# Cross-attention on one core: the order of all steps written anew

## The chip, the cores and the metric
The kernel runs on one core of a Trainium2 chip. The core has five engines, which each work through their own instructions in order and wait for each other by semaphores: TensorE (PE in the profile; its weight loads are PEld), VectorE (DVE), ScalarE (ACT), GpSimd (POOL) and SyncE (SP), which here only issues DMAs. The metric is the device time of one execution in microseconds; the median of several runs counts. Times of single instructions come from one further execution, taken with the hardware profiler.

## The reference
```python
B, C1, C2, N = (8, 512, 512, 1024)
D = C2 // 8
q = jnp.einsum('bcn,dc->bnd', x1, Wq) + bq
k = jnp.einsum('bcn,dc->bdn', x2, Wk) + bk[:, None]
v = jnp.einsum('bcn,dc->bdn', x2, Wv) + bv[:, None]
attn = jax.nn.softmax(jnp.einsum('bnd,bdm->bnm', q, k), axis=2)
attn_out = jnp.einsum('bcm,bnm->bcn', v, attn)
return attn_out + x1
```
All in float32. There are eight batches with 1024 query positions n, 1024 context positions m, 512 channels c and 64 dimensions d.

## The kernel before
Each float32 product that matters is made of three passes in a faster format: a tensor is cut into a high part (h), a low part (l) and a combined difference (d), and TensorE multiplies the matching parts into one PSUM bank, with a rescaling of the bank by ScalarE between the passes h, l and the pass d. So each step of the mathematics has a ScalarE and a VectorE step or two around its matmuls.

The work is written as small methods of a class `Batch`, each of which issues one or a few instructions on one engine. A batch has two halves of 512 queries, four quarters Q of 256 queries and eight blocks u of 128 queries; the context is cut into eight tiles i, j or m of 128. The methods, with their lines:

- `ldx1`, `ldx2` (L157 to L170) load the inputs on SP's queue. `Q`, `K` (L205) project; `qe`, `ke` take the results out, `qd`, `kc` copy them to the other partitions by DMA, `qr`, `ql`, `kr`, `kl` split them.
- `S.h.i` (L262, PE) makes the scores of a half and a tile, `Sc.h.i` (L267, ACT) takes them out into the tile `e`.
- `F.Q` (L275 to L278, DVE) folds the scores of a quarter over its tiles, `T.Q` (L282, POOL) takes the maximum over the partitions (`top`), `L.u` (L290, DVE) subtracts it, `E.u` (L293, ACT) takes the exponential in place.
- `H.u` (L297, ACT), `l.u` (L301, DVE) and `d.u` (L306, DVE) split the exponentials of a block into `eh`, `el`, `ed`.
- The softmax's denominator: `es.Q` (L312, ACT) copies half of a quarter's exponentials, `a1.Q` (L315, a DMA issued by POOL) adds the other half to it, `a2.Q` and `a3.Q` (L319, DVE) fold the rest, `tot.Q` (L329, POOL) sums over the partitions into `den`, `few.Q` (L334, two DMAs on SP's queue) turns a row of it into columns, and `rec.Q` (L338, DVE) takes the reciprocal `r`.
- `xh`, `xl`, `xd` (L352 to L362) split the context, `VX.j`, `vf.j`, `VY.j` (L379, L390) make a tile of v in a bank `ps_v`, `vh`, `vl`, `vd` (L401 to L409) take it out in three parts. `VF` (L372) does two tiles of the first batch in full float32.
- `R.u.m` (L418, PE) adds the passes h and l of block u and tile m to the bank `ps_o`, `fx.u` (L430, ACT) rescales it, `D.u.m` (L418) adds the pass d. `lo.u` (L437, SP) loads the bias into an output tile `o`, `oa.u` (L440, a DMA issued by POOL) adds x1 to it, `ev.u` (L447, DVE) adds the bank times the reciprocal, and `st.u` (L457, SP) stores it. For the very last block of all, `ev.7` does the left half and `ew.7` the right half, with a store each (`st.7`, `sw.7`).

The banks `ps_v` and `ps_o` are five in all (`"B": 5`), used in turn. The first matmul of a new block (`R.u.0`) therefore waits until the `ev` of an older block has read its bank, and that `ev` needs its quarter's reciprocal: `a3`, `tot`, `few`, `rec`, `ev`, `R`, over four engines and a DMA.

Nothing decides the order at run time. Three strings, `FIRST` (batch 0), `MIDDLE` (batches 1 to 6, the same words each time) and `LAST` (batch 7), list the steps as words; a + stands for the next batch, a - for the one before. The function `follow` calls them one after the other, and the place in the string is the place in each engine's queue:
```python
    def follow(words, b):
        for word in words.split():
            at = b + {"-": -1, "+": 1}.get(word[0], 0)
            name, *args = word.lstrip("+-").split(".")
            getattr(states[at], name + "_" * (name in fields))(*map(int, args))
```
The steps that read one tensor from PSUM and at most one from SBUF on VectorE are `vl` (L405) and, beside its output tile, `ev` (L447); `rec` reads one small SBUF tensor; all others of VectorE (L275 to L278, L290, L301, L306, L319, L357, L362, L409) read SBUF alone, and two tensors of it.

Of the kernel before, what the change touches and what calls it, by code (L numbers as in the profile page):

```python
# [27 lines left out]


FIRST = """  # L30
wh.0 VF.1.0 wl.0 ldx2.0 wd.0 ldx2.1 wh.1 VF.0.0 VF.1.1 VF.0.1 VF.0.2 wl.1 VF.1.2 xh.1 w4.0 w4.1 xh.2 VF.0.3 xl.1
lwq vf.0 vh.0 VF.1.3 VX.2 xh.3 VX.3 xl.3 vf.1 vh.1 K ldx1.0 xl.2 wd.1 vl.1 vf.2 ldx1.1 Q vf.3 ke kc vl.0 lo.0
xd.1 vd.0 qe xd.2 VX.4 VY.2 qd kr VX.5 kl VY.3 +ldx1.1 vh.2 xd.3 vl.2 vf.4 qr VY.4 vf.5 vh.4 VY.5 vh.3 ql vh.5
S.0.3 Sc.0.3 vl.3 S.0.2 Sc.0.2 S.0.1 S.0.5 vl.4 Sc.0.5 vl.5 S.0.0 Sc.0.1 vd.2 S.0.7 S.0.4 S.1.7 S.1.5 Sc.0.0
S.0.6 Sc.0.4 Sc.0.7 Sc.0.6 F.0 S.1.4 T.0 S.1.0 Sc.1.4 +ldx1.0 S.1.3 vd.1 S.1.1 Sc.1.1 L.0 Sc.1.7 Sc.1.0 +Q L.1
+ldx2.0 S.1.2 E.0 oa.0 +ldx2.1 Sc.1.5 VX.7 E.1 H.0 F.1 vf.7 Sc.1.3 l.0 S.1.6 H.1 VX.6 Sc.1.6 VY.7 R.0.0 R.0.1
es.0 R.0.2 d.0 l.1 T.1 R.0.3 R.0.4 L.3 R.0.5 L.2 vf.6 Sc.1.2 R.1.0 vh.7 VY.6 R.1.1 R.1.2 +qe lo.1 E.3 H.3 d.1
R.1.3 +K E.2 a1.0 es.1 F.2 vl.7 R.1.4 R.1.5 +qd l.3 vh.6 vl.6 H.2 R.3.0 R.3.1 R.3.2 R.3.3 T.2 lo.2 oa.2 lo.3
a1.1 a2.0 R.1.6 R.1.7 R.0.6 R.0.7 fx.1 L.4 E.4 a3.0 H.4 fx.0 oa.1 +qr l.2 F.3 D.1.0 L.5 tot.0 R.2.0 R.2.1 R.3.4
R.2.2 l.4 R.2.3 R.2.4 R.2.5 R.2.6 E.5 few.0 R.2.7 T.3 a2.1 fx.2 d.3 D.0.0 R.3.5 R.3.6 D.0.1 D.0.2 D.0.3 D.0.4  # L40
+ql R.3.7 fx.3 R.4.0 R.4.1 D.1.1 R.4.2 vd.3 L.6 d.2 D.1.2 D.0.5 D.1.3 +ke es.2 D.1.4 D.1.5 D.0.6 a3.1 D.0.7 E.6
rec.0 R.4.3 R.4.4 R.4.5 H.5 R.4.6 H.6 D.2.0 tot.1 D.2.1 D.2.2 R.4.7 fx.4 d.4 D.3.0 D.3.1 D.3.2 D.3.3 D.3.4 +xh.0
ev.0 D.2.3 D.2.4 D.2.5 l.6 D.3.5 R.6.0 a1.2 R.6.1 D.4.0 D.4.1 D.4.2 D.3.6 D.2.6 D.3.7 D.1.6 D.1.7 +kc R.6.2
R.6.3 +kr L.7 E.7 oa.3 l.5 few.1 +kl ev.1 H.7 d.5 R.6.4 R.6.5 st.0 +S.0.7 l.7 +S.0.4 es.3 lo.4 R.5.0 R.6.6 a1.3
D.2.7 +S.0.6 R.5.1 R.5.2 R.6.7 +Sc.0.4 rec.1 ev.3 +Sc.0.7 +S.0.2 R.5.3 +Sc.0.2 +S.0.1 R.5.4 a2.2 a3.2 tot.2
+Sc.0.6 +xh.1 st.1 D.4.3 +S.0.3 +xl.0 ev.2 +xd.0 a2.3 +xl.1 fx.6 +S.0.5 d.6 a3.3 +Sc.0.3 R.7.0 +Sc.0.1 R.7.1
R.5.5 R.5.6 R.5.7 st.3 +VX.1 few.2 +S.0.0 +Sc.0.0 D.4.4 D.4.5 D.4.6 D.4.7 d.7 +S.1.6 D.6.0 oa.4 st.2 fx.5 rec.2
+Sc.0.5 +F.0 D.5.0 tot.3 lo.6 few.3 lo.5 D.5.1 oa.6 D.5.2 +xh.2 R.7.2 D.5.3 D.5.4 R.7.3 R.7.4 D.5.5 R.7.5 lo.7
R.7.6 D.5.6 D.6.1 D.6.2 +T.0 +S.1.0 D.6.3 +Sc.1.6 ev.4 R.7.7 fx.7 +VX.0 +L.0 +S.1.5 +L.1 D.7.0 D.7.1 rec.3 D.6.4
+vf.0 D.5.7 D.6.5 D.6.6 +F.1 oa.5 oa.7 +xl.2 D.6.7 ev.6 +xh.3 +xl.3 ev.5 +vf.1 +E.0 D.7.2 +E.1 st.4 D.7.3 D.7.4  # L50
D.7.5 D.7.6 D.7.7 +VY.0
"""
MIDDLE = """
VY.1 Sc.1.0 es.0 S.1.4 T.1 +ldx1.0 VX.3 -ev.7 xd.1 H.0 -st.7 l.0 vh.1 S.1.1 vl.1 vh.0 H.1 Sc.1.5 VX.5 vf.3 VX.2
xd.3 VY.3 vh.3 VX.4 Sc.1.4 L.3 S.1.3 Sc.1.1 vf.5 vf.2 +ldx1.1 xd.2 Sc.1.3 S.1.7 S.1.2 vl.0 VY.5 a1.0 +Q Sc.1.2
l.1 E.3 vf.4 L.2 -st.6 VY.2 E.2 lo.1 VY.4 Sc.1.7 vh.5 vd.0 vl.3 -st.5 F.2 VX.6 vh.2 H.3 lo.0 vl.5 VX.7 vh.4 l.3
R.1.0 vl.4 vl.2 +ldx2.1 lo.3 T.2 vf.6 +qe R.3.0 +ldx2.0 R.3.1 R.0.0 R.3.2 vf.7 VY.6 a2.0 R.3.3 H.2 L.5 l.2 VY.7
vd.2 R.1.1 oa.1 R.0.1 R.3.4 L.4 vh.6 R.1.2 vd.1 +K E.4 H.4 a3.0 vl.6 R.0.2 d.3 R.0.3 es.1 oa.3 d.0 tot.0 R.1.3
vh.7 vl.7 vd.3 +qd F.3 R.3.5 R.3.6 R.1.4 R.1.5 +qr R.3.7 R.1.6 R.1.7 oa.0 R.0.4 R.0.5 E.5 es.2 R.0.6 d.1 R.0.7
R.2.0 R.2.1 R.2.2 fx.3 l.4 D.3.0 fx.1 H.5 R.2.3 R.2.4 few.0 +ql D.1.0 R.4.0 a1.2 +ke a2.2 a1.1 a3.2 R.4.1 a2.1  # L60
D.1.1 D.1.2 D.1.3 D.1.4 D.1.5 D.1.6 D.1.7 T.3 L.7 a3.1 fx.0 D.0.0 D.0.1 E.7 L.6 E.6 H.6 D.0.2 D.0.3 R.4.2 R.4.3
l.5 D.0.4 +kc D.0.5 D.3.1 D.3.2 D.3.3 R.2.5 R.2.6 tot.1 rec.0 R.4.4 ev.1 R.4.5 R.4.6 R.5.0 D.3.4 D.3.5 D.3.6
D.3.7 R.2.7 +kr es.3 a1.3 st.1 D.0.6 few.1 R.5.1 d.2 l.6 D.0.7 +kl H.7 R.5.2 +S.0.0 R.5.3 fx.2 +S.0.4 +xh.0 lo.2
d.4 l.7 ev.0 +Sc.0.4 rec.1 D.2.0 oa.2 R.4.7 +Sc.0.0 R.5.4 fx.4 ev.3 lo.4 +S.0.2 tot.2 D.2.1 D.2.2 D.2.3 +S.0.3
+S.0.5 +Sc.0.2 +S.0.7 st.0 +Sc.0.3 +Sc.0.7 +S.0.1 oa.4 a2.3 +Sc.0.1 D.4.0 R.5.5 R.5.6 R.5.7 R.6.0 d.6 +Sc.0.5
+S.1.6 +S.0.6 few.2 D.4.1 fx.5 D.4.2 D.4.3 R.6.1 +xl.0 +Sc.0.6 +F.0 D.2.4 st.3 D.2.5 +T.0 R.6.2 d.5 D.2.6 D.2.7
+VX.1 +xd.0 R.6.3 R.6.4 R.6.5 D.4.4 D.4.5 R.6.6 R.6.7 a3.3 lo.5 ev.2 +L.0 D.4.6 D.4.7 +vf.1 st.2 +xh.1 lo.6
R.7.0 +L.1 +Sc.1.6 +S.1.0 tot.3 rec.2 ev.4 d.7 oa.5 +F.1 R.7.1 R.7.2 R.7.3 R.7.4 R.7.5 fx.6 +xh.2 +xl.2 lo.7
D.5.0 +xh.3 R.7.6 +S.1.5 oa.6 D.5.1 oa.7 R.7.7 fx.7 +VX.0 +vf.0 D.6.0 D.6.1 D.6.2 D.6.3 D.6.4 D.6.5 D.5.2 D.5.3
D.6.6 D.6.7 st.4 D.5.4 +xl.3 D.5.5 +xl.1 D.5.6 few.3 D.5.7 D.7.0 D.7.1 rec.3 ev.6 ev.5 D.7.2 +VY.0 D.7.3 +E.1  # L70
D.7.4 D.7.5 +E.0 D.7.6 D.7.7
"""
LAST = """
xd.1 -st.5 T.1 L.3 es.0 H.0 H.1 L.2 -ev.7 xd.2 VX.5 S.1.2 a1.0 Sc.1.5 VY.1 Sc.1.0 Sc.1.2 S.1.7 xd.3 S.1.1 vh.0
E.3 vf.5 S.1.4 -st.6 vh.1 VX.2 l.1 Sc.1.7 Sc.1.1 vf.2 VY.5 lo.0 vl.1 -st.7 S.1.3 vl.0 E.2 Sc.1.4 es.1 l.0 VX.3
lo.3 Sc.1.3 VX.6 VY.2 vf.3 a2.0 H.2 vh.5 vd.0 VX.4 vf.6 F.2 vl.5 T.2 VY.3 vh.2 vh.3 a1.1 vl.2 VY.6 vf.4 VX.7
VY.4 R.0.0 R.0.1 F.3 H.3 R.0.2 vl.3 l.3 vh.6 vf.7 vl.6 a3.0 l.2 vh.4 vl.4 VY.7 R.3.0 R.3.1 R.1.0 R.1.1 R.3.2
R.3.3 R.3.4 L.5 vh.7 vl.7 tot.0 L.4 E.5 R.1.2 R.1.3 R.0.3 d.1 lo.1 a2.1 lo.2 R.3.5 R.2.0 T.3 E.4 es.2 R.0.4
R.0.5 R.0.6 R.0.7 oa.3 L.7 E.7 oa.1 d.2 a3.1 H.5 d.0 R.1.4 vd.1 R.1.5 l.5 L.6 R.1.6 R.2.1 R.3.6 R.1.7 H.4 fx.0
R.2.2 R.2.3 R.2.4 R.2.5 R.2.6 oa.0 few.0 R.2.7 fx.2 R.3.7 d.3 R.5.0 vd.2 R.5.1 vd.3 oa.2 R.5.2 fx.1 tot.1 D.1.0  # L80
few.1 fx.3 D.0.0 l.4 D.0.1 D.0.2 D.0.3 D.2.0 D.1.1 D.3.0 D.3.1 D.3.2 D.2.1 rec.1 D.3.3 E.6 es.3 D.0.4 D.3.4 H.6
l.6 R.5.3 D.0.5 D.0.6 D.0.7 D.3.5 rec.0 D.2.2 D.3.6 H.7 ev.0 D.3.7 a1.2 D.2.3 D.1.2 D.1.3 D.2.4 D.2.5 R.6.0
D.2.6 ev.3 D.1.4 st.0 a1.3 a2.2 a3.2 R.6.1 D.1.5 st.3 D.1.6 R.5.4 D.1.7 ev.1 st.1 R.5.5 R.5.6 D.2.7 lo.5 tot.2
R.6.2 ev.2 few.2 R.4.0 R.6.3 R.6.4 R.4.1 R.4.2 oa.5 a2.3 d.6 R.5.7 fx.5 lo.6 a3.3 R.4.3 d.5 R.4.4 R.6.5 R.6.6
R.6.7 l.7 st.2 R.4.5 R.4.6 lo.7 lo.4 d.4 oa.6 tot.3 few.3 R.4.7 fx.4 rec.2 D.5.0 D.5.1 D.5.2 D.5.3 D.5.4 d.7
R.7.0 D.5.5 R.7.1 R.7.2 R.7.3 R.7.4 rec.3 R.7.5 R.7.6 fx.6 D.4.0 D.5.6 D.6.0 R.7.7 oa.7 D.4.1 D.4.2 D.5.7 ev.5
fx.7 oa.4 st.5 D.4.3 D.4.4 D.4.5 D.4.6 D.6.1 D.7.0 D.7.1 D.7.2 D.4.7 ev.4 st.4 D.7.3 D.7.4 D.7.5 D.7.6 D.7.7
D.6.2 D.6.3 ew.7 sw.7 ev.7 st.7 D.6.4 D.6.5 D.6.6 D.6.7 ev.6 st.6
"""


# [432 lines left out]
```

## Time and profile before

| | us |
|---|---|
| runs: median (lowest to highest of 3) | 667.14 (665.84 to 667.75) |
| the profiled execution's time | 663.9 |
| its span, first to last instruction | 662.1 |
| TensorE busy | 651.1 |
| VectorE busy | 573.0 |
| ScalarE busy | 401.7 |
| GpSimd busy | 207.2 |

The profile names a group of instructions by its line, engine, operation and tiles (out<-in). Busy times overlap between engines; the time is set by whatever the last instruction waited for, step by step. An engine's idle time costs nothing unless another engine waits for it. A span on POOL is rough. The granted clock is TensorE's share of full speed. Times in the timeline count from the span's start.

### The profile page before, as it was taken

How to read it: one execution, taken by the hardware profiler on the slowest of the kernel's cores; microseconds unless marked ns; L12 is line 12 of the kernel's file. 1: busy time of each engine (PE TensorE's matmuls, PEld its weight loads, DVE VectorE, ACT ScalarE, POOL GpSimd, SP SyncE). 2: the span in 40 equal slices, each digit the busy share in tenths (PEclk: the TensorE clock that was granted, in tenths of full speed). 3: DMA queues.
4: the chain of work that ended last, by engine and by line, in shares of the span. 5: the costliest groups of instructions: out<-in, count | busy, mean ns of one | idle time of the engine just before them, and what ended most of it. 6: DMA issues, size and time to landing. Idle time of an engine off the chain costs nothing. (4 is left out here: it accounts for less than half of the span.)

```text
span 662.1 us, 8012 instructions
## 1 busy us (share of the span) xinstructions
PE 651.1 (98%) x2817; PEld 496.6 (75%) x2817; DVE 573.0 (87%) x661; ACT 401.7 (61%) x565; POOL 207.2 (31%) x164
## 2 busy tenths in 40 slices
...
GB/s 320 188 167 136 84 164 253 228 98 127 149 235 190 96 159 165 185 193 104 149 189 176 192 101 160 205 187 165 113 139 234 183 154 113 141 186 38 73 154 155
DMA packets 50551, 106.73 MB, mean 161 GB/s; under 512 B 14160, under 2 KB 14928, under 8 KB 46800
## 3 DMA queue, kind: packets, MB, share of 16 engines
...
q14 instruction: 17, 0.14, 0.1%
...
## 5 line engine op out<-in xcount | busy, mean ns | idle before, releaser
L418 PE MATMUL ps_o<-vh,eh 128*128 128x512 f32 x512 | 200.9, 392 | 5.6 <-DVE o L447 5.6
L418 PE MATMUL ps_o<-vl,el 128*128 128x512 f32 x512 | 200.0, 391 | 0.0
L418 PE MATMUL ps_o<-vd,ed 128*128 128x512 f32 x512 | 141.0, 393 | 0.2 <-DVE vd L409 0.2
L418 PEld LDWEIGHTS ps_o<-vh,eh 128*128 128x128 f32 x512 | 96.3, 188 | 31.8 <-issue 11.7
L418 PEld LDWEIGHTS ps_o<-vd,ed 128*128 128x128 f32 x512 | 96.5, 189 | 21.8 <-DVE vd L409 0.6
L418 PEld LDWEIGHTS ps_o<-vl,el 128*128 128x128 f32 x512 | 96.4, 188 | 20.4 <-DVE el L301 0.2
L282 POOL PARTITION_ALL_REDUCE top<-max x32 | 50.9, 1589 | 190.8 <-DVE max L278 190.8
L329 POOL PARTITION_ALL_REDUCE den<-es x32 | 77.4, 2420 | 95.9 <-DVE es L319 81.8
L301 DVE TENSOR_TENSOR el<-e,eh 128x1024 fp32r<-128x1024 f32 x64 | 86.7, 1355 | 15.2 <-ACT eh L297 15.1
L440 POOL DMA_DIRECT2D o<-in_x1T_dram x64 | 58.3, 949 | 98.1 <-DMA o<-in_bv_dram 83.7
L267 ACT COPY e<-ps_s 128x512 f32<-128x512 f32 x128 | 71.6, 591 | 28.1 <-PE ps_s L262 27.2
L306 DVE SCALAR_TENSOR_TENSOR ed<-eh,el 128x1024 fp32r<-128x1024 f32 x64 | 83.1, 1306 | 1.1 <-PE ps_o L418 1.1
L430 ACT ACTIVATE ps_o<-ps_o 128x512 f32<-128x512 f32 x64 | 37.1, 585 | 74.3 <-PE ps_o L418 74.1
L290 DVE TENSOR_TENSOR e<-e,top 128x1024 f32<-128x1024 f32 x64 | 80.6, 1272 | 1.5 <-POOL top L282 1.5
L293 ACT ACTIVATE e<-e 128x1024 f32<-128x1024 f32 x64 | 66.9, 1056 | 24.2 <-DVE e L290 24.1
L401 ACT ACTIVATE vh<-ps_v 128x512 fp32r<-128x512 f32 x64 | 37.4, 598 | 58.7 <-PE ps_v L379 58.6
L297 ACT ACTIVATE eh<-e 128x1024 fp32r<-128x1024 f32 x64 | 67.4, 1058 | 1.3 <-DVE ed L306 0.7
L379 PE MATMUL ps_v<-wh,xh 128*128 128x512 f32 x248 | 66.9, 391 | 0.0
L379 PE MATMUL ps_v<-wl,xl 128*128 128x512 f32 x248 | 66.3, 389 | 0.0
L379 PE MATMUL ps_v<-wd,xd 128*128 128x512 f32 x248 | 65.4, 392 | 0.0
L447 DVE SCALAR_TENSOR_TENSOR o<-ps_o,r,o 128x512 f32<-128x512 f32 (+1 forms) x65 | 47.5, 740 | 17.5 <-PE ps_o L418 13.2
L390 ACT ACTIVATE ps_v<-ps_v 128x512 f32<-128x512 f32 x64 | 37.2, 593 | 35.6 <-PE ps_v L379 35.4
...
## 6 DMA issues: line engine op xcount, KB each, us to landing
...
```

Source lines behind the costliest of these rows:

```text
L267: nc.scalar.copy(self.half[h][:, :, i, :], self.ps[h, i].rearrange("p (q n) -> p q n", q=2))
L282: nc.gpsimd.partition_all_reduce(self.top[Q], self.fold[Q][:, 0, :], P, ReduceOp.max)
L290: nc.vector.tensor_tensor(e, e, top, ALU.subtract)
L293: nc.scalar.activation(self.unit(u), self.unit(u), AF.Exp)
L297: nc.scalar.activation(self.e[u]["h"], self.unit(u), AF.Copy, scale=SPLIT)
L301: nc.vector.tensor_tensor(self.e[u]["l"], self.unit(u), f32(self.e[u]["h"]), ALU.subtract)
L306: nc.vector.scalar_tensor_tensor(e["d"], f32(e["h"]), -1.0 / T, f32(e["l"]), ALU.mult, ALU.add)
L329: nc.gpsimd.partition_all_reduce(self.den[Q], self.es[Q][:, 0, :], P, ReduceOp.add)
L379: nc.tensor.matmul(self.B[j], self.c[j // 2][z][:, c, ts(j % 2, P)], w[z][:, c, :], start=(start and c == 0), stop=(stop and c == CT - 1), ...
L418: nc.tensor.matmul(self.B[u], self.e[u][z][:, m, :], self.v[m // 2, z][:, m % 2, :], start=start, stop=stop, skip_group_check=True,)
L440: nc.gpsimd.dma_start(self.o[u], x1T[self.b, ts(u, P), :], accum_op=ALU.add)
L447: nc.vector.scalar_tensor_tensor(o, self.B[u][:, at], self.share(u), o, ALU.mult, ALU.add)
```

## The change
All three strings are laid out anew. The set of steps, the methods and the buffers are the same; each engine gets the same instructions in another order. The aim of the new order by its description: the sums and maxima over the partitions (`tot`, `T` on GpSimd) soon meet a step of VectorE that reads PSUM, or a gap. A line of each string:
```diff
 FIRST = """
-wh.0 VF.1.0 wl.0 ldx2.0 wd.0 ldx2.1 wh.1 VF.0.0 VF.1.1 VF.0.1 VF.0.2 wl.1 VF.1.2 xh.1 w4.0 w4.1 xh.2 VF.0.3 xl.1
+VF.0.0 VF.0.1 VF.1.0 VF.1.1 ldx2.0 lwq VF.0.2 ldx2.1 wh.0 wl.0 VF.1.2 wd.0 VF.1.3 wh.1 ldx1.0 w4.0 wl.1 xh.1
...
 LAST = """
-R.2.2 R.2.3 R.2.4 R.2.5 R.2.6 oa.0 few.0 R.2.7 fx.2 R.3.7 d.3 R.5.0 vd.2 R.5.1 vd.3 oa.2 R.5.2 fx.1 tot.1 D.1.0
+fx.1 H.6 l.5 R.5.0 R.5.1 D.1.0 oa.3 tot.1 d.3 D.1.1 D.3.0 fx.0 D.1.2 D.3.1 D.3.2 vd.2 L.7 E.7 vd.3 D.1.3 es.3
```
What the engines get is seen at three places. Names there carry the batch, then the block, quarter or pair of tiles, then a running number: `den_7_1` is the denominator of quarter 1 in batch 7, `r_7_1` its reciprocal, `el_7_5` the low part of block 5.

VectorE in the last batch, from the addition that releases the sum of quarter 1 (the second L319) to the reciprocal that needs this sum. Before:
```order
L319 TENSOR_TENSOR es_7_1_4970<-es_7_1_4970 128x256
L306 SCALAR_TENSOR_TENSOR ed_7_0_5148<-eh_7_0_4896,el_7_0_4972 128x1024
L409 TENSOR_TENSOR vd_7_1_5152<-vh_7_1_5030,vl_7_1_5034 128x1024
L301 TENSOR_TENSOR el_7_5_5156<-e_7_1_4789,eh_7_5_5146 128x1024
L290 TENSOR_TENSOR e_7_1_4789<-e_7_1_4789,top_7_3_5126 128x8x128
L306 SCALAR_TENSOR_TENSOR ed_7_3_5189<-eh_7_3_5064,el_7_3_5069 128x1024
L409 TENSOR_TENSOR vd_7_2_5194<-vh_7_2_5003,vl_7_2_5022 128x1024
L409 TENSOR_TENSOR vd_7_3_5198<-vh_7_3_5071,vl_7_3_5074 128x1024
L301 TENSOR_TENSOR el_7_4_5212<-e_7_1_4789,eh_7_4_5167 128x1024
L338 RECIPROCAL r_7_1_5223<-few_7_1_5207 128x2
```
Now:
```order
L319 TENSOR_TENSOR es_7_1_5019<-es_7_1_5019 128x256
L409 TENSOR_TENSOR vd_7_1_5163<-vh_7_1_5001,vl_7_1_5026 128x1024
L338 RECIPROCAL r_7_0_5175<-few_7_0_5160 128x2
L301 TENSOR_TENSOR el_7_5_5185<-e_7_1_4787,eh_7_5_5153 128x1024
L306 SCALAR_TENSOR_TENSOR ed_7_3_5196<-eh_7_3_5073,el_7_3_5075 128x1024
L409 TENSOR_TENSOR vd_7_2_5204<-vh_7_2_5024,vl_7_2_5040 128x1024
L290 TENSOR_TENSOR e_7_1_4787<-e_7_1_4787,top_7_3_5091 128x8x128
L409 TENSOR_TENSOR vd_7_3_5208<-vh_7_3_5013,vl_7_3_5021 128x1024
L301 TENSOR_TENSOR el_7_6_5217<-e_7_1_4787,eh_7_6_5183 128x1024
L338 RECIPROCAL r_7_1_5228<-few_7_1_5225 128x2
L319 TENSOR_TENSOR es_7_2_5132<-es_7_2_5132 128x512
L319 TENSOR_TENSOR es_7_2_5132<-es_7_2_5132 128x256
```
The reciprocal of quarter 0 has moved from behind that of quarter 1 to the second place after the addition, and the additions of quarter 2 have moved ahead of the first `ev` of the batch.

GpSimd around the same sum. Before:
```order
L440 DMA o_7_3_4983<-in_x1T_dram 128x512
L440 DMA o_7_1_5116<-in_x1T_dram 128x512
L440 DMA o_7_0_4959<-in_x1T_dram 128x512
L440 DMA o_7_2_5119<-in_x1T_dram 128x512
L329 ISA den_7_1_5204<-es_7_1_4970 128x256
L315 DMA es_7_2_5129<-e_7_1_4789 128x1024
```
Now:
```order
L440 DMA o_7_1_4913<-in_x1T_dram 128x512
L440 DMA o_7_3_4958<-in_x1T_dram 128x512
L329 ISA den_7_1_5194<-es_7_1_5019 128x256
L315 DMA es_7_2_5132<-e_7_1_4787 128x1024
L440 DMA o_7_0_4915<-in_x1T_dram 128x512
L440 DMA o_7_2_5171<-in_x1T_dram 128x512
```
Two of the four output DMAs have moved behind the sum; the accumulating DMA of quarter 2 still follows it.

VectorE after the same addition in a middle batch (batch 2). Before:
```order
L319 TENSOR_TENSOR es_2_1_1815<-es_2_1_1815 128x256
L290 TENSOR_TENSOR e_2_1_1464<-e_2_1_1464,top_2_3_1908 128x8x128
L301 TENSOR_TENSOR el_2_5_1926<-e_2_1_1464,eh_2_5_1877 128x1024
L338 RECIPROCAL r_2_0_1941<-few_2_0_1883 128x2
L447 SCALAR_TENSOR_TENSOR o_2_1_1687<-ps_o_2_1_1734,r_2_0_1941,o_2_1_1687 128x512
```
Now:
```order
L319 TENSOR_TENSOR es_2_1_1774<-es_2_1_1774 128x256
L301 TENSOR_TENSOR el_2_5_1934<-e_2_1_1462,eh_2_5_1897 128x1024
L255 TENSOR_TENSOR kl_3_1940<-k_3_1862,kh_3_1938 128x1024
L306 SCALAR_TENSOR_TENSOR ed_2_4_1946<-eh_2_4_1830,el_2_4_1832 128x1024
L338 RECIPROCAL r_2_0_1953<-few_2_0_1873 128x2
L447 SCALAR_TENSOR_TENSOR o_2_0_1807<-ps_o_2_0_1748,r_2_0_1953,o_2_0_1807 128x512
```
The subtraction of the maximum (L290) has moved away, and the splits of the next batch's k (L255) and of block 4 (L306) have moved in ahead of the reciprocal. At the very end, the left and right halves of block 7 (`ev.7`, `ew.7`) are now VectorE's last steps, and `ev.6`, which was last, stands ahead of the `ev` of blocks 5, 4 and 7.

More of the change, by code (lines that the diff above doesn't have):

```diff
@@ L30 @@
 FIRST = """
-wh.0 VF.1.0 wl.0 ldx2.0 wd.0 ldx2.1 wh.1 VF.0.0 VF.1.1 VF.0.1 VF.0.2 wl.1 VF.1.2 xh.1 w4.0 w4.1 xh.2 VF.0.3 xl.1
[L32 to L50, printed above, removed]
@@ new lines @@
+D.3.4 D.3.5 R.4.1 R.4.2 +ke a2.1 d.2 R.4.3 R.4.4 R.4.5 tot.0 vd.3 few.0 R.4.6 L.5 fx.1 D.0.3 D.0.4 D.2.0 D.0.5
+D.0.6 H.6 D.2.1 D.2.2 D.0.7 +kc l.6 +xh.0 rec.0 E.5 R.4.7 a3.1 D.1.0 D.1.1 D.1.2 D.1.3 D.1.4 D.1.5 D.1.6 D.2.3
+es.2 oa.2 H.5 ev.0 L.7 fx.4 E.7 d.4 st.0 D.1.7 R.6.0 D.2.4 D.3.6 tot.1 ev.1 R.6.1 R.6.2 R.6.3 R.6.4 R.6.5 R.6.6
++kr l.5 a1.2 +xl.0 R.5.0 D.2.5 D.4.0 R.5.1 D.3.7 R.6.7 D.2.6 few.1 H.7 +xh.1 R.5.2 R.5.3 D.4.1 d.6 es.3 oa.3
+R.5.4 +kl +S.0.7 d.5 fx.6 +Sc.0.7 +S.0.5 R.5.5 D.2.7 st.1 D.6.0 +S.0.6 +Sc.0.5 a2.2 +xh.3 a3.2 +Sc.0.6 +S.0.3
```

80 lines of the change are left out of this document (47 added, 33 removed).

## The prediction
> **What bounds the kernel now.** I read the engines' shares first, then stretches of the span, then TensorE's waits, and last the order in time around the one large wait. The first line of the page:
> ```profile
> PE 651.1 (98%) x2817; PEld 496.6 (75%) x2817; DVE 573.0 (87%) x661; ACT 401.7 (61%) x565; POOL 207.2 (31%) x164
> ```
> TensorE (PE) is busy for 651.1 of 662.1 us, so all that a new order can win lies in the other 11.0 us and in matmuls that run at a low clock. The table of stretches says where they are (its columns: length, then busy us and count for PE, PEld, DVE, ACT and POOL, granted clock, DMA share, GB/s):
> ```profile
> 0.00:20.00 20.00, 19.02 (x59) 8.96 (x61) 9.23 (x11) 11.73 (x16) 0.19 (x4) 1.00 0.78 275
> 200.00:300.00 100.00, 100.00 (x439) 75.21 (x436) 88.23 (x101) 63.09 (x88) 30.34 (x26) 1.00 0.65 166
> 629.20:634.80 5.60, 0.00 (x0) 0.03 (x1) 2.29 (x5) 0.47 (x1) 0.04 (x1) 0.95 0.79 148
> 634.80:638.10 3.30, 3.30 (x9) 2.63 (x10) 1.54 (x3) 0.00 (x0) 1.63 (x1) 0.57 0.45 160
> ```
> In a middle stretch PE is busy for 100.00 of 100.00 us at full clock. In the last batch it stands still for 5.60 us, and after that it runs for 3.30 us at a clock of 0.57. The list of PE's waits agrees (us in total, times, longest):
> ```profile
> PE ps_o L418 <- DVE o L447: 5.6, 1, 5.6
> PE ps_warm L473 <- DVE spark L468: 1.0, 1, 1.0
> PE ps_o L418 <- DVE vd L409: 0.2, 1, 0.2
> ```
> So there is one wait worth having: a matmul of line 418 waits for VectorE's `ev` (line 447) to free a PSUM bank. From 612 to 635 us the timelines of GpSimd (POOL), VectorE (DVE) and SyncE's queue (SPq) read thus (start, length, what, and in brackets the idle time before it):
> ```profile
> 616.11 10.58 POOL L329 PARTITION_ALL_REDUCE den<-es  x1 [1.83 <-issue]
> ```
> ```profile
> 615.53 0.41 DVE L319 TENSOR_TENSOR es<-es 128x256 f32<-128x256 f32 x1
> 615.87 1.21 DVE L306 SCALAR_TENSOR_TENSOR ed<-eh,el 128x1024 fp32r<-128x1024 f32 x1
> 617.00 1.21 DVE L409 TENSOR_TENSOR vd<-vh,vl 128x1024 fp32r<-128x1024 f32 x1
> 618.13 1.21 DVE L301 TENSOR_TENSOR el<-e,eh 128x1024 fp32r<-128x1024 f32 x1
> ...
> 623.81 1.21 DVE L301 TENSOR_TENSOR el<-e,eh 128x1024 fp32r<-128x1024 f32 x1
> 632.40 0.17 DVE L338 RECIPROCAL r<-few 128x2 f32<-128x2 f32 x1 [7.38 <-DMA few<-den]
> 632.50 1.23 DVE L301 TENSOR_TENSOR el<-e,eh 128x1024 fp32r<-128x1024 f32 x1
> 633.65 0.16 DVE L338 RECIPROCAL r<-few 128x2 f32<-128x2 f32 x1
> 633.91 1.41 DVE L447 SCALAR_TENSOR_TENSOR o<-ps_o,r,o 128x512 f32<-128x512 f32 x2
> ```
> ```profile
> 626.71 1.12 SPq L334 DMA_DIRECT2D few<-den  x2
> ```
> The sum over the partitions of quarter 1 (`tot.1`, line 329) takes 10.58 us. Beside it VectorE issues eight steps without a gap (from 615.87 to 623.81 are seven steps of 1.13 us, the distance of 617.00 and 618.13), and each reads two SBUF tensors. The last of them begins at 623.81 and ends at 625.02; the sum ends at 626.69, 1.67 us later. Then the chain runs to PE: `few` is issued at 626.71, the reciprocal starts at 632.40, `ev` at 633.91, PE at 634.80. How long the same step takes elsewhere (min/median/max in ns):
> ```profile
> L329 POOL PARTITION_ALL_REDUCE den<-es x32: 1786/2064/10580, 58.4 to 646.4; - x32
> L282 POOL PARTITION_ALL_REDUCE top<-max x32: 1056/1746/1965, 37.1 to 609.4; - x32
> ```
> I take 1.79 us as the sum's own time, so this one came 10.58 - 1.79 = 8.79 us late. It seems to have got SBUF only when VectorE ran dry. PE waited 5.60 us for a result that came 8.79 us late: without the delay it would have come 3.2 us before PE needed it. That is the cushion there.
>
> **The change, part by part.** No instruction is added or removed; only the order differs. Durations are from this profiled execution: span 662.1 us, time 663.9, so 1.8 lie around the span. The median of the runs is 667.14, 3.2 above it; I carry the difference over to the median.
>
> *The sum of quarter 1 in the last batch.* Now one `vd` (line 409) follows the addition that releases it, and then a reciprocal (`rec.0`), which does not hold two SBUF tensors. If that lets GpSimd in, the sum waits for one step only. What this costs is shown in the middle of the program, where a sum came while a two-tensor step (line 290) was running:
> ```profile
> 148.81 2.70 POOL L329 PARTITION_ALL_REDUCE den<-es  x1 [5.73 <-DVE es L319]
> ```
> ```profile
> 148.64 1.22 DVE L290 TENSOR_TENSOR e<-e,top 128x1024 f32<-128x1024 f32 x1
> 149.78 2.12 DVE L301 TENSOR_TENSOR el<-e,eh 128x1024 fp32r<-128x1024 f32 x1
> ```
> The sum took 2.70 us, 0.91 more than 1.79, and the next VectorE step 2.12, 0.90 more than 1.22. So the sum ends 10.58 - 2.70 = 7.9 us earlier. PE's wait was 5.6: all of it goes, with 7.9 - 5.6 = 2.3 to spare. Gain **5.6 us**.
>
> *The slow clock behind the wait.* In 3.30 us at 0.57 the work of 1.88 us was done. Without the standstill there is no reason for it: 3.30 x 0.43 = **1.4 us**. The Trainium skill, "TensorE: Matmul & The Clock Gate", section "What's actually happening", has the array at half clock until it was busy for a window of about 3.4 us; by that page's figure, an estimate, the term would be 1.7.
>
> *What is late next there.* In the new order two additions (`a2.2`, `a3.2`) stand between `rec.1` and the `ev` that frees the bank for block 6, and they wait for the accumulating DMA `a1.2`, which GpSimd issues only after the sum:
> ```profile
> 626.56 0.93 POOL L315 DMA_DIRECT2D es<-e  x1
> ...
> DMA to landing us min/median/max: 4.6/6.4/7.7
> 635.23 1.14 DVE L319 TENSOR_TENSOR es<-es 128x512 f32<-128x512 f32 x2
> ```
> From the end of the addition that releases the sum: 2.7 (sum) + 6.4 (DMA) + 1.1 (two additions) + 0.75 (`ev`) + 0.14 (633.91 + 0.75 = 634.66 to PE's 634.80) = 11.1 us, and 9.3 to 12.4 by the ends of the DMA's range. In the old order that addition ended at 615.94 and PE stood at this matmul at 629.20, 13.3 us later; if PE comes as late now, even 12.4 is hidden. Cost 0; were PE there 2 us sooner, up to 1.1.
>
> *The middle batches.* A meeting there costs either engine about 0.9 us (148.81), and VectorE has 100 - 88.23 = 11.8 us idle in 100. PE there has nothing to give (100.00 busy), so a better meeting of GpSimd and VectorE brings 0. New waits bound it from the other side: the old order had 0.2 us in all, and I take 0, with up to 0.3 in each of the eight batches = 2.4 for the range.
>
> *The start and the end.* The first 20 us hold 0.98 us of PE's idle time, ahead of the warm-up matmuls, which don't move. The end swaps the last output step:
> ```profile
> 656.57 0.88 DVE L447 SCALAR_TENSOR_TENSOR o<-ps_o,r,o 128x256 f32<-128x256 f32 x2
> 657.93 0.75 DVE L447 SCALAR_TENSOR_TENSOR o<-ps_o,r,o 128x512 f32<-128x512 f32 x1 [0.49 <-PE ps_o L418]
> ```
> Two halves of block 7 (0.88) now stand last in place of the whole block 6 (0.75): +0.1, with a store of half the size behind it. I take 0.
>
> Sum: 5.6 + 1.4 = 7.0. Against its own time 663.9 - 7.0 = 656.9; at the median 667.14 - 7.0 = **660.1 us**. What ties the runs closer than 0.3% (2 us) I hold for no change.
>
> **The rivals.**
>
> *The slot is missed.* If the sum starts after `rec.0` has gone by, six two-tensor steps follow (lines 301, 306, 409, 290, 409, 301), until `rec.1`, which waits for this very sum. It is then 6 x 1.13 = 6.8 us later than forecast; less the 13.3 - 11.1 = 2.2 left above, PE waits 4.6, and 1.4 of slow clock come back: 660.1 + 6.0 = 666. For it: one step between the release and `rec.0` is a slot of 1.1 us. Against it: GpSimd started 0.17 us after the release at 615.94.
>
> *The long sum was one unlucky draw.* At 148.81 GpSimd came in at the first boundary though another two-tensor step followed at once, and the longest maximum, 1.97 us, is the shortest one's 1.06 and 0.91 more; only the eight steps at 615.87 did not let go. If the timed runs mostly lack it, the order is worth nothing there: 667. Against it: they are 3.2 us slower than the profiled one, not faster. The Trainium skill, "SBUF — State Buffer", section "Who interferes with whom", says that a VectorE step with two SBUF inputs contends with a GpSimd step that reads SBUF and that whoever issues first has the port for the whole instruction. By that rule a sum should lose one step; the trace agrees at 148.81 (0.91 us) and not at 616.11 (seven boundaries lost).
>
> *Slower: the middle batches get the same wait.* There `tot.1` is now followed by lines 301, 255 and 306 ahead of the reciprocal, where lines 290 and 301 stood. If it loses all of these, it is 2 x 1.13 = 2.3 us later than at its first boundary. With a cushion like the 3.2 above nothing happens; below 2.3 - 7.0 / 7 = 1.3 us of cushion in each of seven batches the gain is gone, and with none the time is 660.1 + 7 x 2.3 = 676. Against it: of 64 such steps one was starved; a step that waits (line 301 had 15.1 us of waits for ScalarE in all) opens a gap.
> ```profile
> DVE el L301 <- ACT eh L297: 15.1, 12, 1.9
> ```
>
> **How the numbers follow.** Forecast as summed: 0.74. Small new waits in the middle (to +2.4, 662.5): 0.10. Slot missed (666): 0.05. Unlucky draw (667): 0.06. Slower (about 669 to 676): 0.05. The first two are faster by over 0.3%, which is below 665.1: 0.84. The next two are within 0.3%: 0.11. Slower: 0.05. The range begins at 655.0: the sum against the profiled execution, 656.9, less the spread of the runs shown (665.84 to 667.75, 1.9 us). It ends at 664.0, which is the small waits' 662.5 and most of that spread again. Outside lie the last three cases, 0.16.
>
> **What would show it.** Right: no wait of `ps_o` L418 for `o` L447 in the list of PE's waits, the largest L329 under 2.8 us, the clock 1.00 in all stretches after 20 us, span about 655. Slot missed: one L329 of 7 to 10 us near the end and PE's wait at about 5. Unlucky draw: the wait is gone from the profile, and the times stay at 667. Slower: L329 over 4 us in several batches and PE waits that recur every 80 us. The forecast is wrong too if another stage, the stores or the last reciprocal behind `few.3`, ends last in place of PE.

## The result, and the profile after

| | before | after |
|---|---|---|
| median of the runs, us (lowest to highest of 4) | 666.49 (664.82 to 667.75) | 655.40 (654.65 to 656.37) |
| ratio of the times, 95% interval | | 0.9835 (0.9812 to 0.9859) |
| the profiled execution's time, us | 663.9 | 656.37 |
| its span, us | 662.1 | 654.6 |
| granted clock over the span | 0.997 | 1.000 |

The new order is faster by 11.1 us between the medians and by 7.5 us between the profiled executions. The forecast was 660.1 with a range of 655.0 to 664.0: the direction is right, and the time lies 4.7 below the number and only 0.4 above the low end of the range.

The engines' shares after, from the head of the page:
```profile
PE 648.5 (99%) x2817; PEld 495.3 (76%) x2817; DVE 563.3 (86%) x661; ACT 400.2 (61%) x565; POOL 195.3 (30%) x164
```
TensorE's (PE's) idle time fell from 11.0 to 654.6 - 648.5 = 6.1 us, and its busy time by 2.6 us. The stretches after (length, then busy us and count for PE, PEld, DVE, ACT and POOL, granted clock, DMA share, GB/s):
```profile
0.00:20.00 20.00, 19.02 (x61) 8.26 (x63) 9.12 (x10) 11.68 (x16) 0.19 (x4) 1.00 0.75 277
200.00:300.00 100.00, 100.00 (x439) 75.12 (x440) 88.93 (x105) 62.66 (x87) 31.97 (x27) 1.00 0.66 169
629.00:640.00 11.00, 11.00 (x50) 9.08 (x49) 9.73 (x12) 1.16 (x2) 1.77 (x1) 1.00 0.60 184
640.00:654.60 14.60, 10.75 (x48) 8.57 (x46) 3.21 (x6) 1.16 (x2) 3.92 (x5) 1.00 0.71 161
```
The third row is the place of the old standstill: PE is busy for all of it, at full clock. What PE still waits for (us in total, times, longest):
```profile
PE ps_warm L473 <- DVE spark L468: 1.0, 1, 1.0
PE ps_q L205 <- DMA x<-in_x_dram: 1.0, 1, 1.0
PE ps_o L418 <- DVE el L301: 0.3, 1, 0.3
```
The 5.6 us are gone, and one wait of 1.0 us is new: the projection Q of the next batch's x1, at 121.70, for its load. The sum over the partitions and the maximum, over the whole program (min/median/max in ns), and the last batch on GpSimd and VectorE (start, length, what, and the idle time before it):
```profile
L329 POOL PARTITION_ALL_REDUCE den<-es x32: 1786/2110/2697, 63.0 to 638.2; - x32
L282 POOL PARTITION_ALL_REDUCE top<-max x32: 1056/1281/1965, 36.7 to 605.9; - x32
```
```profile
615.56 2.63 POOL L329 PARTITION_ALL_REDUCE den<-es  x1 [6.07 <-DVE es L319]
618.06 0.92 POOL L315 DMA_DIRECT2D es<-e  x1
```
```profile
615.32 1.22 DVE L409 TENSOR_TENSOR vd<-vh,vl 128x1024 fp32r<-128x1024 f32 x1
616.45 0.16 DVE L338 RECIPROCAL r<-few 128x2 f32<-128x2 f32 x1
616.95 1.62 DVE L301 TENSOR_TENSOR el<-e,eh 128x1024 fp32r<-128x1024 f32 x1 [0.34 <-ACT eh L297]
618.49 1.21 DVE L306 SCALAR_TENSOR_TENSOR ed<-eh,el 128x1024 fp32r<-128x1024 f32 x1
...
623.03 1.21 DVE L301 TENSOR_TENSOR el<-e,eh 128x1024 fp32r<-128x1024 f32 x1
625.84 0.17 DVE L338 RECIPROCAL r<-few 128x2 f32<-128x2 f32 x1 [1.60 <-DMA few<-den]
625.92 1.13 DVE L319 TENSOR_TENSOR es<-es 128x512 f32<-128x512 f32 x2
626.97 1.40 DVE L447 SCALAR_TENSOR_TENSOR o<-ps_o,r,o 128x512 f32<-128x512 f32 x2
```
The sum of quarter 1 takes 2.63 us in place of 10.58. It runs while `vd` (line 409) ends, `rec.0` goes by and VectorE idles for 0.34 us; the next step is 1.62 us long where 1.21 is usual. The sum ends at 618.19, where it ended at 626.69.

### The profile page after: what moved, and what is told of

It reads as the page before. It is cut to its first block, busy times and chain, and to the rows that moved or that the text cites. A ratio compares the mean times of both kernels' runs of the same rounds, so it can differ in the third digit from the quotient of the medians.

```text
span 654.6 us, 7991 instructions
## 1 busy us (share of the span) xinstructions
PE 648.5 (99%) x2817; PEld 495.3 (76%) x2817; DVE 563.3 (86%) x661; ACT 400.2 (61%) x565; POOL 195.3 (30%) x164
## 4 chain that ended last, share of the span: by engine, by line
PE 86%; DMA 1%; DVE 1%; issue 0%; ACT 0%; DVEq 0%
PE ps_o L418 49%; PE ps_v L379 22%; PE ps_s L262 8%; PE ps_q L205 3%; PE ps_k L205 3%; DMA x<-in_x_dram 1%; DVE o L447 0%; DVE e L290 0%; DVE el L301 0%; ACT vh L401 0%; ACT ps_v L390 0%; DVEq L520 0%; DVE es L319 0%; DVE ed L306 0%
## 5 line engine op out<-in xcount | busy, mean ns | idle before, releaser
L418 PE MATMUL ps_o<-vd,ed 128*128 128x512 f32 x512 | 139.2, 389 | 0.0
L329 POOL PARTITION_ALL_REDUCE den<-es x32 | 72.4, 2263 | 105.6 <-DVE es L319 94.1
L267 ACT COPY e<-ps_s 128x512 f32<-128x512 f32 x128 | 70.1, 593 | 49.5 <-PE ps_s L262 49.1
L290 DVE TENSOR_TENSOR e<-e,top 128x1024 f32<-128x1024 f32 x64 | 88.7, 1388 | 7.7 <-POOL top L282 7.7
L282 POOL PARTITION_ALL_REDUCE top<-max x32 | 44.6, 1395 | 154.5 <-DVE max L278 106.3
L301 DVE TENSOR_TENSOR el<-e,eh 128x1024 fp32r<-128x1024 f32 x64 | 79.4, 1241 | 0.5 <-ACT eh L297 0.3
L306 DVE SCALAR_TENSOR_TENSOR ed<-eh,el 128x1024 fp32r<-128x1024 f32 x64 | 78.1, 1229 | 0.3
L379 PEld LDWEIGHTS ps_v<-wd,xd 128*128 128x128 f32 x248 | 44.9, 188 | 16.7 <-issue 4.9
```

What stands on the lines that cost most here:

```text
L267: nc.scalar.copy(self.half[h][:, :, i, :], self.ps[h, i].rearrange("p (q n) -> p q n", q=2))
L290: nc.vector.tensor_tensor(e, e, top, ALU.subtract)
L301: nc.vector.tensor_tensor(self.e[u]["l"], self.unit(u), f32(self.e[u]["h"]), ALU.subtract)
L306: nc.vector.scalar_tensor_tensor(e["d"], f32(e["h"]), -1.0 / T, f32(e["l"]), ALU.mult, ALU.add)
L329: nc.gpsimd.partition_all_reduce(self.den[Q], self.es[Q][:, 0, :], P, ReduceOp.add)
L379: nc.tensor.matmul(self.B[j], self.c[j // 2][z][:, c, ts(j % 2, P)], w[z][:, c, :], start=(start and c == 0), stop=(stop and c == CT - 1), ...
```

## The experiments

The theory is that this one sum is the gain, since GpSimd gets in only where VectorE stops holding two SBUF inputs. The rivals are that the long sum is a draw that other executions may miss, and that other parts of the new order bring the time. "The sum" below is always `tot.1` of the last batch. Medians of kernels that ran side by side are compared; the kernel before had medians of 665.48, 664.47, 665.20 and 666.00 beside them.

**The kernel before, again.** No edit.

> The kernel before, unchanged, profiled a second time: is the long sum of quarter 1 in the last batch a property of the order or a draw? Theory (order): eight two-input VectorE steps without a gap start behind the addition again, so the sum again takes 9 to 12 us and PE waits 5 us or more once, on L418 <- L447. Rival (draw): the sum gets in at one of the eight boundaries, takes 2 to 8 us, and PE waits anything from 0 to 5.

Measured: 667.32 us, span 665.6. The sum (GpSimd's timeline), PE's largest waits, and PE alone in the stretches behind the stop:
```profile
618.08 10.58 POOL L329 PARTITION_ALL_REDUCE den<-es  x1 [1.83 <-issue]
```
```profile
PE ps_o L418 <- DVE o L447: 5.6, 1, 5.6
PE ps_v L379 <- DVE o L447: 1.2, 1, 1.2
```
```profile
636.00:640.00 4.00, 3.24 (x8) 2.60 (x9) 2.29 (x4) 0.00 (x0) 1.57 (x1) 0.51 0.37 133
640.00:645.00 5.00, 5.00 (x18) 3.96 (x17) 2.21 (x4) 0.00 (x0) 0.22 (x1) 0.71 0.24 82
```
The sum is as long as before, to the hundredth, so it is no draw. What does vary is the price of the stop: 3.24 x 0.49 + 5.00 x 0.29 = 3.0 us are lost to the clock, where the first profile had 1.4. The clocks 0.57, 0.51 and 0.71 are means over stretches. The traces behind the profiles record the granted clock itself: it is 0.5 for 3.41 us in the first profile and for 6.83 us, twice as long, in this one, and 1.0 on both sides. And a second wait of 1.2 us, in batch 1, which the first profile lacks, came on top. These two make 1.6 + 1.2 = 2.8 of the 3.5 us between the two spans.

**One reciprocal moved in the old order.**
```diff
-... a3.1 H.5 d.0 R.1.4 vd.1 R.1.5 l.5 ...
+... a3.1 H.5 d.0 few.0 rec.0 R.1.4 vd.1 R.1.5 l.5 ...
-R.2.2 ... R.2.6 oa.0 few.0 R.2.7 ...
+R.2.2 ... R.2.6 oa.0 R.2.7 ...
-... D.3.5 rec.0 D.2.2 ...
+... D.3.5 D.2.2 ...
```

> The kernel before with one reciprocal of quarter 0 (and the DMAs it needs) moved to right behind the first two-input step after the addition; nothing else differs. Theory (this one sum is the whole gain): the sum takes about 2.7 us in place of 10.6, PE's wait of 5.6 us is gone, the stretch runs at clock 1.00, the span is 662.1 - 7.0 = 655.1; in the timed runs the kernel is level with the changed one, about 656, if the 3.2 us by which the timed runs exceed the profiled one belong to the same stall, and about 659.5 (666.5 - 7.0) if they don't. Rival (the middle batches or other parts of the new order bring it): the wait may go, but the time stays at 662 or above. Rival (draw): nothing changes but by chance, 666.

Measured: 657.02 us (656.51 to 658.03), ratio 0.9875 (0.9856 to 0.9894); span 655.2, clock 1.000. GpSimd, then VectorE, then the head of the page:
```profile
616.39 2.63 POOL L329 PARTITION_ALL_REDUCE den<-es  x1 [1.83 <-issue]
```
```profile
616.15 1.22 DVE L306 SCALAR_TENSOR_TENSOR ed<-eh,el 128x1024 fp32r<-128x1024 f32 x1
617.28 0.15 DVE L338 RECIPROCAL r<-few 128x2 f32<-128x2 f32 x1
617.36 2.04 DVE L409 TENSOR_TENSOR vd<-vh,vl 128x1024 fp32r<-128x1024 f32 x1
```
```profile
PE 649.9 (99%) x2817; PEld 495.9 (76%) x2817; DVE 574.0 (88%) x661; ACT 401.7 (61%) x565; POOL 198.8 (30%) x164
```
GpSimd comes in at the reciprocal, and the step behind it pays 0.8 us. The span is the expected 655.1 within 0.1. The timed runs fell by 8.5 us, more than the 6.9 between the spans: with the stop, the excess of the timed runs over the profiled one has gone too.

The `ev` that PE waits for in the old order is that of block 0. It needs the reciprocal of quarter 0, not the late sum; it only stands behind `rec.1` in VectorE's queue (the rows at 632.40, 633.65 and 633.91 of the kernel before). This edit leaves `ev.0` behind `rec.1`, so its gain does come through the shorter sum. To move `rec.0` and `ev.0` ahead of `rec.1` would be another way to spare PE the wait; no run tries it.

**A gap early, and a gap late.** A VectorE step of 0.06 us that reads no SBUF, in the old order, once behind the second of the eight two-input steps and once behind the fifth:
```diff
+        def gap(self):
+            nc.vector.memset(spark, 0.0)
-... d.0 R.1.4 vd.1 R.1.5 ...
+... d.0 R.1.4 vd.1 gap R.1.5 ...        (early)
-... R.3.7 d.3 R.5.0 vd.2 ...
+... R.3.7 d.3 gap R.5.0 vd.2 ...        (late)
```

> The kernel before with one added VectorE step that reads no SBUF (a memset of one column, about 0.06 us) behind the second of the eight two-input steps. Theory (GpSimd waits only for a VectorE step that does not hold two SBUF inputs): the sum ends about 1.8 us after that step, 6.8 us earlier than before, PE's wait is gone, span 655 to 656, and the time as with the moved reciprocal. Rival (a boundary alone decides, the step's kind does not): so short a step is no opening, the sum still takes about 10.6 us, and the time stays at 666.

> The same added step, but behind the fifth of the eight two-input steps: a dose between none and the early gap. Theory: the sum takes about 7.2 us, ends 3.4 us earlier than before, and PE still waits 5.6 - 3.4 = 2.2 us; a stop so short may or may not lower the clock, so the span is 662.1 - 3.4 = 658.7 with the slow clock and 657.3 without. Rival (the sum gets in wherever it happens to): its length has nothing to do with the place of the step.

Measured, early: 656.82 us (656.58 to 658.44), ratio 0.9873 (0.9854 to 0.9893), span 655.3. Late: 660.33 us (658.88 to 661.53), ratio 0.9921 (0.9900 to 0.9942), span 658.4. Lines are higher by 3 here (L332 is the sum, L183 the added step). The early one on GpSimd and VectorE:
```profile
615.51 3.77 POOL L332 PARTITION_ALL_REDUCE den<-es  x1 [1.83 <-issue]
```
```profile
617.54 2.10 DVE L304 TENSOR_TENSOR el<-e,eh 128x1024 fp32r<-128x1024 f32 x1
617.56 0.06 DVE L183 MEMSET spark<- 128x1 f32 x1
```
The late one on GpSimd and VectorE, and PE's wait:
```profile
616.61 7.17 POOL L332 PARTITION_ALL_REDUCE den<-es  x1 [1.83 <-issue]
```
```profile
622.05 2.10 DVE L412 TENSOR_TENSOR vd<-vh,vl 128x1024 fp32r<-128x1024 f32 x1
622.07 0.06 DVE L183 MEMSET spark<- 128x1 f32 x1
```
```profile
PE ps_o L421 <- DVE o L450: 2.2, 1, 2.2
```
The sum ends 1.7 us after the added step in both (619.28 and 623.78), and PE's wait follows it: 0, then 2.2, against 5.6 with no gap. This is the expected dose to a tenth of a microsecond. So in the old order one sum costs PE's wait, and a single short VectorE step, put early enough, ends it.

**The reciprocal late in the new order, and the gap closed.** In the changed kernel `rec.0` goes back behind the row of two-input steps; in the second kernel `vd.2` also closes the idle 0.3 us.
```diff
-... few.0 vd.1 R.0.4 ... R.3.7 rec.0 R.0.6 ...
+... few.0 vd.1 R.0.4 ... R.3.7 R.0.6 ...             (second kernel: vd.1 vd.2)
-... D.3.3 few.1 rec.1 ...
+... D.3.3 rec.0 few.1 rec.1 ...
```

> The changed kernel with the reciprocal of quarter 0 in the last batch moved from the second place after the addition to behind the last step of the run, ahead of the reciprocal of quarter 1. What stays in its place is an idle 0.3 us, in which VectorE waits for ScalarE's high part of block 5. Theory (GpSimd waits until VectorE does not hold two SBUF inputs, by a small step or by idling): the sum still takes about 2.7 us, no wait of PE on L447, time as the changed kernel's, 655.4. Rival (the small step itself is needed): the sum takes 9 us or more, PE waits 6 to 7 us, 663 or above.

> As the kernel with the late reciprocal, and the third tile pair's line 409 is moved up to close the idle 0.3 us: seven two-input VectorE steps then follow the addition without a gap, in the changed order. Theory (the gap is the whole gain): the sum ends about 6.8 us later than in the changed kernel, where almost no cushion was left, so PE waits about 6.9 us on L418 <- L447; with 1.4 to 3.0 us of slow clock behind the stop the time is 655.4 + 6.9 + 1.4 to 3.0 = 663.7 to 665.3. Rival (the rest of the new order carries the gain): the time stays below 659. Rival (a draw): the sum gets in at one of the first boundaries and the time stays at 655.4.

Measured: 656.25 us (654.45 to 657.22), ratio 0.9868 (0.9843 to 0.9894), with the idle time left; 655.35 us (654.93 to 656.08), ratio 0.9856 (0.9833 to 0.9878), with the gap closed. VectorE with the idle time left, then with the gap closed, where GpSimd's row follows:
```profile
615.98 1.61 DVE L301 TENSOR_TENSOR el<-e,eh 128x1024 fp32r<-128x1024 f32 x1 [0.42 <-ACT eh L297]
```
```profile
615.02 3.25 DVE L409 TENSOR_TENSOR vd<-vh,vl 128x1024 fp32r<-128x1024 f32 x2
618.20 1.21 DVE L301 TENSOR_TENSOR el<-e,eh 128x1024 fp32r<-128x1024 f32 x1
```
```profile
615.27 2.63 POOL L329 PARTITION_ALL_REDUCE den<-es  x1 [6.07 <-DVE es L319]
```
The kernel before has two such steps at 621.54:
```profile
621.54 2.35 DVE L409 TENSOR_TENSOR vd<-vh,vl 128x1024 fp32r<-128x1024 f32 x2
```
Here the theory falls in its strong form. Two steps of line 409 follow each other without a gap (the pair takes 3.25 us, where two take 2.35), and GpSimd came in between them. In the new order neither the reciprocal nor the idle time was needed.

**The changed kernel again, and one load earlier.** The first is unchanged; the second issues `+ldx1.0` ahead of the store `-st.7` in the middle batches, where it stood two stores later.
```diff
-... Sc.1.0 -st.7 vf.5 ... vf.6 +ldx1.0 +Q vl.5 ...
+... Sc.1.0 +ldx1.0 -st.7 vf.5 ... vf.6 +Q vl.5 ...
```

> The changed kernel unchanged, timed again on the same chip as the others, to compare it with the one moved reciprocal (657.0 there). Theory (this sum is nearly the whole gain, the rest of the new order gives 0 to 1 us): 655 to 656.5, a ratio of 0.983 to 0.987, and a profile with a wait of PE for the x load near 1 us. Rival (the rest of the order gives 2 us or more): 655 or below in most runs, ratio under 0.984.

> The changed kernel with the load of the second half of the next batch's x1 issued ahead of the store of the previous batch's block 7 in the middle batches, where it stood behind two stores that wait for their output steps. It is meant to remove the one wait of 1.0 us that the new order added (the first matmul of Q for the load near 120 us). If the load then starts 3 us or more earlier, the wait goes and the time falls by up to 1.0 us, to about 654.4; if the load shares the DMA engines with the loads and stores around it and lands no sooner, or the store delays an output tile, it stays at 655.4 or rises.

Measured: 655.38 us (655.07 to 655.59), ratio 0.9858 (0.9839 to 0.9876), span 653.5; with the load earlier 654.77 us (654.30 to 655.99), ratio 0.9852 (0.9831 to 0.9873), span 652.9. In this profile of the unchanged kernel the wait for the load is absent, so it comes in some executions only, and the earlier load can't be told from no change: 0.6 us between medians whose runs overlap. It is the lowest median of all, by that much.

What the rest of the new order is worth is read against the old order with its one reciprocal moved, which has neither the stop nor the wait for the load. PE does the same 2817 matmuls in 648.4 us here, and in 649.9 there; the spans are 653.5 and 655.2. The passes d of line 418 differ most (busy us, mean ns; old order with the reciprocal moved, then the changed kernel):
```profile
L418 PE MATMUL ps_o<-vd,ed 128*128 128x512 f32 x512 | 140.5, 392 | 0.2 <-DVE vd L409 0.2
```
```profile
L418 PE MATMUL ps_o<-vd,ed 128*128 128x512 f32 x512 | 139.2, 389 | 0.0
```
A pair of profiles alone would not show that the order does it: the old order with the early gap was busy for only 649.0 us. The middle batches do show it. From the first score matmul (line 262) of batch 2 to that of batch 6 PE runs 1408 matmuls without idle time at full clock. By the traces they take 321.55 to 321.65 us in all seven profiles of the old order and 320.96 in all seven of the new: about 0.16 us a batch. What makes them denser stays open. In the timed runs a difference was not separated: the ratios 0.9875 and 0.9858, from different chips, have overlapping intervals.

**Why the old order keeps the sum out.** Four kernels look for what the old order has and the new one lacks. In the first, the old order, two of the output DMAs go behind the sum:
```diff
-... R.2.6 oa.0 few.0 ... vd.3 oa.2 R.5.2 fx.1 tot.1 D.1.0
+... R.2.6 few.0 ... vd.3 R.5.2 fx.1 tot.1 oa.0 oa.2 D.1.0
```

> The kernel before with two of GpSimd's output DMAs (quarter 0's and 1's blocks 0 and 2 in the last batch) moved from ahead of the sum to behind it, as the new order has them; VectorE's order is untouched, so the eight two-input steps still stand without a gap. If the DMAs that GpSimd issues just ahead of the sum are what let VectorE keep it out, the sum now gets in at the first boundary and takes 2.7 us, with no wait of PE. If the row of VectorE's steps alone decides, it still takes 9 to 10.6 us and PE waits 5 us or more.

In the second, the first two of the eight steps of the old order change places:
```diff
-... H.5 d.0 R.1.4 vd.1 R.1.5 ...
+... H.5 vd.1 R.1.4 d.0 R.1.5 ...
```

> The kernel before with the first two of the eight two-input steps behind the addition in the other order: line 409 first, line 306 second. The row is as long and as tight as before. In the changed order with its gap closed, line 409 came first and the sum got in at the first boundary. If the kind of the step that runs when the sum arrives decides, the sum now takes 2.7 us and PE's wait goes; if it doesn't, 9 to 10.6 us and a wait of 5 us or more.

In the new order with the gap closed, line 306 goes first, and in a last kernel two more ready steps join the row:
```diff
-... few.0 vd.1 vd.2 R.0.4 ...
+... few.0 d.3 vd.1 vd.2 R.0.4 ...              (last kernel: d.3 vd.1 vd.2 vd.3 L.7)
```

> The changed order with the gap closed as before, and with line 306 of block 3 moved to the first place after the addition, ahead of the two steps of line 409: the first two steps are now of the kinds that stand first in the kernel before, and GpSimd's DMAs are behind the sum. If the kinds of the first steps decide, the sum is kept out for some six boundaries, PE waits 6 to 7 us and the time is 663 or above; if GpSimd's DMAs ahead of the sum decide, or a detail of the old order that is in neither, the sum takes 2.7 us and the time is 655 to 656.

> The kernel with line 306 first and the gap closed, and two more two-input steps that are ready by then (line 409 of the last pair of tiles, line 290 of block 7) moved up behind the first three, so that VectorE has four ready two-input steps behind the running one when the sum arrives, where it had two and then one that still waits for ScalarE; two matmuls of block 5 stand three matmuls later to make room. In the kernel before, all the steps behind the running one were ready early. If the number of ready steps decides whether GpSimd is kept out, the sum is kept out for four boundaries or more, takes 6 us or more, and with almost no cushion PE waits and the time goes to 659 to 665. If it doesn't, the sum takes 2.7 us and the time stays at 655 to 656, and why the old order alone keeps it out stays open.

Measured: 662.93 us with the DMAs behind the sum and 665.08 with the steps swapped (one run each); 655.92 us (654.99 to 656.55), ratio 0.9860 (0.9833 to 0.9887), with line 306 first; 656.96 us (656.25 to 657.53), ratio 0.9872 (0.9850 to 0.9894), with the longer row. GpSimd in the first two of these four, and PE's wait in the first:
```profile
616.09 10.58 POOL L329 PARTITION_ALL_REDUCE den<-es  x1 [3.61 <-DVE es L319]
```
```profile
PE ps_o L418 <- DVE o L447: 4.3, 1, 4.3
```
```profile
616.84 10.58 POOL L329 PARTITION_ALL_REDUCE den<-es  x1 [1.83 <-issue]
```
With the DMAs moved PE's wait is shorter than the 5 us expected, though the sum is as long: the reciprocal waits 6.10 us for `few` there, in place of 7.38. With the steps swapped it is 5.6. GpSimd with line 306 first, and VectorE there:
```profile
614.23 2.63 POOL L329 PARTITION_ALL_REDUCE den<-es  x1 [6.07 <-DVE es L319]
```
```profile
613.99 1.22 DVE L306 SCALAR_TENSOR_TENSOR ed<-eh,el 128x1024 fp32r<-128x1024 f32 x1
615.12 3.25 DVE L409 TENSOR_TENSOR vd<-vh,vl 128x1024 fp32r<-128x1024 f32 x2
```
VectorE with the longer row, then GpSimd:
```profile
615.72 4.39 DVE L409 TENSOR_TENSOR vd<-vh,vl 128x1024 fp32r<-128x1024 f32 x3
620.03 1.21 DVE L290 TENSOR_TENSOR e<-e,top 128x1024 f32<-128x1024 f32 x1
```
```profile
614.83 2.63 POOL L329 PARTITION_ALL_REDUCE den<-es  x1 [6.07 <-DVE es L319]
```
The longer row took more time than the 655 to 656 us expected, but not by the sum. In the old order both edits leave the sum kept out; in the new order it gets in at the first boundary between two steps in each of the three rows without a gap. The two DMAs ahead of the sum, the kind of the first steps and the number of ready steps, as far as it was raised, are excluded as the sole cause.

The moment at which the sum comes is not excluded. The rows give it alike: 0.24 us after the running step began in the old order (616.11 and 615.87) and in the new (614.23 and 613.99). The traces hold the starts to the nanosecond, and there the two differ. All fourteen profiles together have 203 meetings in which a sum or a maximum starts during a VectorE step with two SBUF inputs and the next such step follows without a gap while it runs. In six of them GpSimd is kept out, and in these the next step starts 894 to 896 ns after GpSimd's: the sum of quarter 1 in the kernel before, in its second profile, with the DMAs moved, with the steps swapped, and in the two kernels with a gap, up to that gap. In the other 197 the next step starts at most 890 ns or 945 to 965 ns after it, and GpSimd comes in there, as the longer next step shows; the three rows of the new order have 887, 889 and 890. The steps of the row follow each other every 1.13 us, so a moment that is bad at one boundary comes again at each of the next, and a step of another length breaks the row. This fits every profile, but the six meetings all belong to one place in the old order, and no run shifts the sum by a few nanoseconds with the order left alone. So it is the rival that is left, not a shown cause.

## Why the prediction was right, and where it was not

- **The sum of quarter 1, 5.6 us.** Right in size and place: the sum was to take 2.70 us and took 2.63, and PE's wait is gone. That this alone carries most of the gain is shown by the one moved reciprocal, which gives 8.5 us in the timed runs, where the whole new order gave 9.1 in its repeat (664.47 to 655.38). The reason given was half right. In the old order a step without two SBUF inputs is enough; in the new order it was not needed, and why is not shown. The Trainium skill, "SBUF — State Buffer", section "Who interferes with whom", would have a sum lose one step to the one that issued first: the new order agrees in every variant (2.63), the old one does not (up to seven boundaries lost, in four profiles).
- **The slow clock, 1.4 us: the term that was too small.** The mechanism is right, and the size was that of one mild execution. Four profiles hold a stop of 4.3 us or more: the clock is at half for 3.41 us in two of them (the kernel before; the DMAs moved) and for 6.83 us in two (its second profile, with 3.0 us lost; the steps swapped). The mean clock was 0.997 in the first two and 0.993 and 0.995 in the others. Of the 32 timed runs of the kernel before beside the experiments 27 have 0.995, as the profile with the long low clock and the steps swapped has, so the long case is probably the usual one: a loss of 0.005 x 663.7 = 3.3 us by this measure, against 0.003 x 662.1 = 2.0 in the first profile. With 3.0 in place of 1.4 the sum is 5.6 + 3.0 = 8.6; the one moved reciprocal gave 8.5.
- **What is late next, 0.** Right, by very little, and along another path than the one summed. The accumulating DMA was put at 6.4 us; by the trace it landed at 625.57, 7.5 us after its issue at 618.06. The two DMAs of `few`, which the sum of this chain leaves out, were ready only at 625.75, and it is for them that the reciprocal at 625.84 waited (1.60 us); the two additions follow it at 625.92, `ev` at 626.97. PE starts this block at 627.77 and hardly waits. That is 12.4 us after the addition that releases the sum ended (614.25 + 1.14 = 615.39), where 11.1 and at most 12.4 were forecast. The cushion that the prediction put at 13.3 - 11.1 = 2.2 us was used up.
- **The middle batches, 0.** The argument that a PE which is busy all the time has nothing to give was wrong: the matmuls stand closer, about 0.16 us a batch in every profile of the new order, and 1.2 us over this pair of profiles (651.1 - 1.4 - 648.5). The allowance for new waits was right in kind: one of 1.0 us came, at a load, not at the sums. The slower rival, a starved sum in several batches, did not happen: the longest sum is 2.70 us.
- **The start and the end, 0.** Right within 0.3 us, which is what is left of the account: 5.6 + 1.4 + 1.2 - 1.0 + 0.3 = 7.5, the difference of the spans.
- **From the profiled execution to the median: the step that failed.** Against its own time the sum gave 656.9, and 656.37 was measured. The text then said of the 3.2 us between the profiled execution and the median: "I carry the difference over to the median." That difference was not a constant. Part of it belonged to the stop, as the longer slow clock (3.3 - 2.0 = 1.3 us by the clocks above), and goes with it: with the one moved reciprocal median and profiled run are both 657.02, and after the change the median lies 1.0 below its profiled run. Part was waits that come and go (the 1.2 us in the second profile). And part was the draw of three runs, whose median was 667.14: the kernel before had medians of 664.47 to 666.00 later, and the profiled execution was one of its fastest. The prediction had noted, against the unlucky draw, that the timed runs were slower than the profiled one; the same row should have raised the gain. That the range still holds the result owes something to luck: its low end was set from the profiled execution's sum, 656.9, less the spread of three runs, and not from this reasoning.
